# SS2D layer: where the weight and background pools are created relative to the tile pools

## The chip, the core and the metric

The kernel runs on one core of a Trainium2 chip. The metric is the device time of one execution in microseconds (us). The core has five engines that run side by side: PE (matrix multiplies), DVE (VectorE), ACT (ScalarE), POOL (GpSimd) and SP, whose queue issues nearly all transfers here.

## What is computed

Four layers in a row on 8 images of 56 x 56 positions with 128 channels. Layers 0, 2 and 3 are deformable convolutions followed by a small MLP. Layer 1 is the one that the change touches, an SS2D block (a selective scan in four directions). Its core, cut from the reference:

```python
def step(h, t):
    dt_t, u_t, B_t, C_t = t
    h = h * jnp.exp(dt_t[..., None] * A) + (dt_t * u_t)[..., None] * B_t[:, :, None, :]
    y = jnp.einsum('bkdn,bkn->bkd', h, C_t)
    return (h, y)
```

Before the scan stand a layer norm, a projection to 256 channels and a gate, a 3 x 3 depthwise convolution and the projections that give dt, B and C; behind it stand a layer norm, the gate, an output projection and an MLP with 512 hidden channels, each with a residual.

## The kernel before

The layers run one after the other. A layer of deformable convolution (class `Dcn`; layers 2 and 3 share one instance) has two parts per image: a *front*, which loads the image (`xt`, L616), transposes it, makes the projected table (L638, stored by L593), the depthwise convolution (`cv`, L657 and L659), offsets and masks (`om`, L670 to L720) and the list of window addresses (`addr`, L725); and the *sampling*, which builds windows of weights (POOL memset of `win`, L803; ACT hats, L749 and L751; POOL `ay`, L760; DVE `patch`, L809, and `win`, L812) and contracts them on PE. While one image is sampled, the front of the next is interleaved. The first image of an instance has nothing to hide behind but what the layer before leaves.

Layer 1 (class `Vss`) cuts each image into 4 directions x 4 chunks of 784 positions: 128 steps in all, 32 units each. A unit holds 32 channels x 4 states on the 128 partitions and does, in this order: `dA` = exp(dt A) on ACT (L1424), `u` = dt u B on DVE (L1434) or, for every fourth unit, `up` on POOL (L1430), the scan `h` on DVE (L1537), `hc` = h C on POOL (L1542), and PE sums over the states (L1456). The tile `dt` (128 x 2 x 784, three buffers) is fetched by SP (L1364) for every four units. Background generators are advanced by a fixed pace between units: `input_stage` prepares the next image, `output_stage` finishes a chunk of 392 positions (L1235 to L1302: two transfers in, PE steps through a single PSUM buffer `misc`, each emptied by ACT, and one store at L1302). In the last image four output stages are still to be done when the last scan ends.

The weights of the SS2D layer are loaded by ten transfers in `Vss.weights` (L1067) and prepared by small DVE and ACT operations (L1075 to L1114).

The order of work follows from tile pools and a scheduler. A pool takes a contiguous part of each partition's on-chip memory (SBUF), in the order in which pools are created; every tag in it gets its buffers there. Pools of a later layer take the same bytes once the earlier layer has left them, so where a pool lies decides for whose last use its successor waits. In the program as built, the relevant byte ranges per partition are, before the change:

| pool | holds | bytes |
|---|---|---|
| `v_img`, `v_prep` | y, xb, dbl, dd, sp, st, out | 9,408 to 75,520 |
| `v_work` | dt (3 x 6,272), b, c, u, h, hc, up | 75,520 to 163,328 |
| `v_const` | the SS2D weights | 163,328 to 191,008 |
| `v_bg` | the tiles of input_stage and output_stage | 191,008 to 224,096 |

and of the instance for layers 2 and 3, which follows on the same bytes: `c_const` and `c_img` (L501, L502) from 9,408 to 75,040; `c_front` (L503: xt, xT, xp, cv, h and small tiles) from 75,040 to 97,056; `c_block` and `c_tail` (sw, xw, st, X, gelu and others) from 97,056 to 160,928; the unit pools (L775: hat, ay, win, patch) from 160,928 on. PSUM pools are the same before and after.

The functions that the diff touches, and those that call them:

Of the kernel before, what the change touches and what calls it, by code (L numbers as in the profile page):

```python
# [41 lines left out]
F32 = mybir.dt.float32  # L42
# [76 lines left out]
SC, SR = 784, 14  # L119
# [367 lines left out]
class Dcn:  # L487
# [9 lines left out]
    def run(self):  # L497
        tc, nc = self.tc, self.nc
        with ExitStack() as ctx:
            enter = ctx.enter_context  # L500
            self.cp = enter(tc.tile_pool(name="c_const", bufs=1))  # L501
            self.img = enter(tc.tile_pool(name="c_img", bufs=1))  # L502
            self.fp = enter(tc.tile_pool(name="c_front", bufs=1))  # L503
            self.bp = enter(tc.tile_pool(name="c_block", bufs=3))
            self.tp = enter(tc.tile_pool(name="c_tail", bufs=1))
            self.pt = enter(tc.tile_pool(name="c_pt", bufs=3, space=PSUM))
            self.py = enter(tc.tile_pool(name="c_py", bufs=2, space=PSUM))
            self.pm = enter(tc.tile_pool(name="c_pm", bufs=3, space=PSUM))
            self.constants()
            for part in self.parts:  # L510
                part.w = self.net.dcn_weights(part.layer, self.const)
                self.part_constants(part)
                self.split_bias(part)
            self.loop()
            self.check()
        over = nc.values_load(self.net.flag[:1, :1], min_val=0, max_val=1, skip_runtime_bounds_check_because="a comparison's result")
        with tc.If(over > 0):
            for part in self.parts:
                self.net.dcn_slow(part.layer, self.images, part.src, part.dst)
# [513 lines left out]
class Vss:  # L1033
# [8 lines left out]
    def run(self):  # L1042
        tc = self.tc
        with ExitStack() as ctx:
            enter = ctx.enter_context
            self.img = enter(tc.tile_pool(name="v_img", bufs=1))
            self.prep = enter(tc.tile_pool(name="v_prep", bufs=1))
            self.work = enter(tc.tile_pool(name="v_work", bufs=2))
            self.cp = enter(tc.tile_pool(name="v_const", bufs=1))
            self.bg = enter(tc.tile_pool(name="v_bg", bufs=1))  # L1050
            self.dram = enter(tc.tile_pool(name="v_dram", bufs=2, space=DRAM))
            self.pmisc = enter(tc.tile_pool(name="v_misc", bufs=1, space=PSUM))
            self.pdtu = enter(tc.tile_pool(name="v_pdtu", bufs=1, space=PSUM))
            self.pda = enter(tc.tile_pool(name="v_pda", bufs=2, space=PSUM))
            self.pacc = enter(tc.tile_pool(name="v_pacc", bufs=1, space=PSUM))
            self.weights()
            self.scans()
# [300 lines left out]

    def fetch_dt(self, s, cg):

        t = s["dt", cg] = self.work.tile([128, 2, SC], F32, name="dt", tag="dt", bufs=3)
        r = s["dd"]
        src = bass.AP(tensor=r.tensor, offset=r.offset + TC * cg * 2 * SC, ap=[[2 * SC, TC], [0, TS], [1, 2 * SC]])
        self.last_fetch = self.nc.sync.dma_start(out=t.rearrange("p x e -> p (x e)"), in_=src)  # L1364
# [274 lines left out]
```

## Time and profile before

| what | us |
|---|---|
| median of three runs (17844.23 to 17852.9) | 17851.06 |
| the profiled execution's own time | 17839.74 |
| its span, first to last instruction | 17838.2 |
| layer 0, up to the flag check | 0 to 2110 |
| first scan and last scan of layer 1 (L1537) | 2218 and 13404 |
| last store of layer 1 (L1302) | 13583 |
| first window memset of layer 2 (L803) | 13586 |
| end of layers 2 and 3 | 17838 |

Between 3000 and 13000 us, in the middle of layer 1, POOL is busy 9384 of 10000 us, DVE 9104, PE 7951 and ACT 6187. In layers 2 and 3 DVE is the busiest engine and POOL has little to do.

How to read it: the page gives busy times per engine and per group of instructions, with the mean duration of one and the idle time of the engine just before them, and what ended that idle time. A line of a timeline gives start, duration, engine, source line, operation, tiles, and in brackets the idle time before it. SPq lines are issues of transfers on SP's queue.

### The profile page before, as it was taken

What the parts mean: (1) busy time and instruction counts of PE and PEld (TensorE: products, weight loads), DVE (VectorE), ACT (ScalarE), POOL (GpSimd) and SP (SyncE); (2) the same over time, 40 slices, a digit from 0 to 9 for tenths busy, and PEclk for the clock granted to TensorE, in tenths of its full rate; (3) what the DMA queues carried; (4) which work ended last, traced back from release to release, by engine and by line L of the source; (5) the groups of instructions that cost most, each with busy time, mean ns of one, the idle gap of its engine ahead of it and who ended that gap; (6) DMA issues with size and microseconds to landing.
All of it is one profiled execution on the core that took longest, in us unless ns stands there. A gap on an engine that the chain in (4) does not pass through costs nothing. (4 is left out here: it accounts for less than half of the span.)

```text
span 17838.2 us, 255485 instructions
## 1 busy us (share of the span) xinstructions
PE 13881.5 (78%) x90058; PEld 6881.4 (39%) x90058; DVE 15386.3 (86%) x17779; ACT 10928.2 (61%) x19607; POOL 11758.9 (66%) x6462
## 2 busy tenths in 40 slices
PE   5777788788788788788778878878776888777777
PEld 3555522232232233232223223223224666555555
DVE  8888488998998998998898899899996888888886
ACT  4666566566566566566666656656554666666666
POOL 2222189998998998998998999899992111122221
PEclk7788898899899899889888888989887888777778
DMA  7777544444343343343444344344434777777777
GB/s 211 211 204 206 165 153 154 172 169 150 143 159 141 139 163 137 139 165 137 143 162 143 137 158 144 140 155 150 148 134 134 199 198 199 196 210 193 209 196 176
DMA packets 1343087, 2961.69 MB, mean 166 GB/s; under 512 B 90960, under 2 KB 893716, under 8 KB 1327420
## 3 DMA queue, kind: packets, MB, share of 16 engines
q1 hardware_dynamic: 1341788, 2945.17, 52.9%
q8 instruction: 718, 11.76, 0.3%
q14 instruction: 581, 4.76, 0.1%
HBM read 2240.63 MB, written 866.92 MB: 174 GB/s over the span
## 5 line engine op out<-in xcount | busy, mean ns | idle before, releaser
L1542 POOL TENSOR_TENSOR hc<-h,c 128x784 f32<-128x784 f32 x4096 | 7539.5, 1874 | 640.9 <-DVE h L1537 387.9
L1537 DVE TENSOR_TENSOR_SCAN h<-dA,st,u 128x784 f32<-128x784 f32 x3072 | 5579.2, 1840 | 438.9 <-ACT dA L1424 243.2
L1424 ACT ACTIVATE dA<-dt,v_A 128x784 f32<-128x784 f32 x4096 | 3741.9, 915 | 842.2 <-DVE h L1537 827.7
L1456 PE MATMUL acc<-hc,v_sum 128*32 128x392 f32 x16384 | 3148.3, 542 | 103.9 <-POOL hc L1542 103.3
L1434 DVE TENSOR_TENSOR u<-dtu,b 128x784 f32<-128x784 f32 x3072 | 2864.6, 957 | 382.5 <-PE dtu L1418 378.4
L1418 PE MATMUL dtu<-dt,ident 128*128 128x392 f32 x4096 | 2028.2, 626 | 1081.9 <-issue 833.4
L760 POOL TENSOR_TENSOR ay<-hat,om 112x756 f32<-112x756 f32 (+2 forms) x192 | 504.6, 2628 | 2848.6 <-ACT hat L751 2309.7
L1537 DVE TENSOR_TENSOR_SCAN h<-dA,st,up 128x784 f32<-128x784 f32 x1024 | 1876.7, 1833 | 232.0 <-POOL hc L1542 208.6
L1430 POOL TENSOR_TENSOR up<-dt,b 128x784 f32<-128x784 f32 x1024 | 1908.1, 1863 | 79.5 <-DVE h L1537 47.1
L845 ACT COPY st<-pt 128x448 f32<-128x448 f32 (+1 forms) x2240 | 1177.4, 542 | 1201.1 <-PE pt L843 1194.6
L812 DVE TENSOR_TENSOR win<-win,patch 112x252 f32 (+2 forms) x3456 | 1686.4, 501 | 132.2 <-POOL win L803 32.5
L1540 ACT COPY st<-h 128x1 f32<-128x1 f32 x3072 | 582.6, 190 | 1985.3 <-DVE h L1537 1976.8
L843 PE MATMUL pt<-ident,sw 112*128 112x112 f32 (+2 forms) x8960 | 1600.6, 308 | 165.6 <-DMA sw<-skew 165.5
L1456 PEld LDWEIGHTS acc<-hc,v_sum 128*32 128x32 f32 x16384 | 762.0, 116 | 2485.3 <-issue 1656.6
L1418 PEld LDWEIGHTS dtu<-dt,ident 128*128 128x128 f32 x4096 | 860.1, 230 | 2150.6 <-issue 1365.5
L803 POOL MEMSET win<- 128x1820 f32 (+2 forms) x384 | 630.0, 1647 | 1298.4 <-DMA skew<-win 1111.2
L859 PE MATMUL yps<-st,xw 128*32 128x48 f32 (+5 forms) x35840 | 1075.2, 244 | 420.7 <-ACT st L845 414.6
L843 PEld LDWEIGHTS pt<-ident,sw 112*128 112x128 f32 (+2 forms) x8960 | 1113.4, 160 | 441.0 <-issue 156.8
L809 DVE TENSOR_TENSOR patch<-ay,hat 112x756 f32<-112x756 f32 (+2 forms) x1152 | 1225.3, 1070 | 39.5 <-POOL ay L760 36.6
L859 PEld LDWEIGHTS yps<-st,xw 128*32 128x32 f32 (+2 forms) x35840 | 754.1, 125 | 849.5 <-ACT st L845 501.0
L749 ACT ACTIVATE hat<-om,taps 112x252 f32<-112x252 f32 x1280 | 758.6, 730 | 277.2 <-DVE patch L809 261.4
L1448 PE MATMUL acc<-y,ident 128*64 128x392 f32 x1536 | 599.1, 780 | 348.6 <-ACT y L1467 269.5
(193 smaller groups left out, 19827.3 us busy)
## 6 DMA issues: line engine op xcount, KB each, us to landing
dt<-dds SPq DMA_DIRECT2D x1024, 784.0 KB
b<-rows SPq DMA_DIRECT2D x512, 392.0 KB
c<-rows SPq DMA_DIRECT2D x512, 392.0 KB
dds<-dd SPq DMA_DIRECT2D x256, 784.0 KB
sw<-skew SPq DMA_DIRECT2D x224, 812.0 KB
sw<-skew SPq DMA_DIRECT2D x224, 672.0 KB
sw<-skew SPq DMA_DIRECT2D x224, 588.0 KB
skew<-win SPq DMA_DIRECT2D x128, 560.0 KB
```

The source lines that it names most:

```text
L809: nc.vector.tensor_mul(patch[:n], bcast(a, 3, KX), bcast(b, 2, KY))
L812: self.last_add = nc.vector.tensor_add(to, to, patch[:n, NCB * p : NCB * (p + 1)]).ins
L843: last = nc.tensor.transpose(ps[:m, n * g : n * (g + 1)], sw[:n, g, p : p + m], self.net.ident[:n, :n])
L845: nc.scalar.copy(st[:m], ps[:m, : G * n])
L859: self.nc.tensor.matmul(yps[CG * g : CG * (g + 1), t0:t1], lhsT=xw[:m, k + part, CG * g : CG * (g + 1)], rhs=st[:m, at + t0 : at + t1], st ...
L1418: last = nc.tensor.matmul(ps[:, b, :SH], lhsT=self.net.ident, rhs=s["dt", cg][:, 1, SH * b : SH * (b + 1)], start=True, stop=True)
L1424: nc.scalar.activation(da[:, :SC], s["dt", cg][:, 0], AF.Exp, scale=w["A"][:, k, NSG * cg + sg : NSG * cg + sg + 1])
L1430: nc.gpsimd.tensor_mul(u, s["dt", cg][:, 1], s["b", sg])
L1434: nc.vector.tensor_mul(halves[0], s["dtu", cg][:, :, :SH], halves[1])
L1456: nc.tensor.matmul(acc[r : r + TC, :SH], lhsT=w["sum"], rhs=hc[:, SH * b : SH * (b + 1)], start=False, stop=sg == NSG - 1)
L1537: nc.vector.tensor_tensor_scan(hh[:, ::step], dA[:, :SC][:, ::step], u[:, ::step], st[:, t : t + 1], ALU.mult, ALU.add)
L1542: nc.gpsimd.tensor_mul(hc, hh, s["c", sg])
```

## The change

A new pool `v_spread` of three buffers is created where `v_work` was, and holds `dt` alone. `v_const` and `v_bg` follow it, and `v_work`, now without dt, comes after them.

```diff
-            self.work = enter(tc.tile_pool(name="v_work", bufs=2))
+            self.spread = enter(tc.tile_pool(name="v_spread", bufs=3))
             self.cp = enter(tc.tile_pool(name="v_const", bufs=1))
             self.bg = enter(tc.tile_pool(name="v_bg", bufs=1))
+            self.work = enter(tc.tile_pool(name="v_work", bufs=2))
...
-        t = s["dt", cg] = self.work.tile([128, 2, SC], F32, name="dt", tag="dt", bufs=3)
+        t = s["dt", cg] = self.spread.tile([128, 2, SC], F32, name="dt", tag="dt")
```

No operation, tile, size or number of buffers is changed, and dt keeps its bytes (75,520 to 94,336). The new ranges are `v_const` 94,336 to 122,016, `v_bg` 122,016 to 155,104, and `v_work` (b, c, u, h, hc, up) 155,104 to 224,096.

## The prediction

> **What bounds the kernel now.** I read the page first (engines over the span, costliest groups), then the busy times by stage, then the timelines of the two places where layer 1 meets its neighbours.
>
> ```profile
> DVE  8888488998998998998898899899996888888886
> POOL 2222189998998998998998999899992111122221
> ...
> L1542 POOL TENSOR_TENSOR hc<-h,c 128x784 f32<-128x784 f32 x4096 | 7539.5, 1874 | 640.9 <-DVE h L1537 387.9
> L1537 DVE TENSOR_TENSOR_SCAN h<-dA,st,u 128x784 f32<-128x784 f32 x3072 | 5579.2, 1840 | 438.9 <-ACT dA L1424 243.2
> L1430 POOL TENSOR_TENSOR up<-dt,b 128x784 f32<-128x784 f32 x1024 | 1908.1, 1863 | 79.5 <-DVE h L1537 47.1
> ```
>
> Slices 6 to 30 are layer 1. POOL and DVE are both at nine tenths there: each unit costs POOL one hc (1874 ns) and a quarter of an up, and DVE one scan and three quarters of a u. They feed each other through three h buffers, so time saved or lost on POOL passes to the span in large part.
>
> ```profile
> 3000.00:13000.00 10000.00, 7951.28 (x28504) 2821.20 (x28506) 9103.87 (x6877) 6187.12 (x10873) 9383.92 (x5182) 0.89 0.42 150
> 13405.00:13585.00 180.00, 131.46 (x597) 87.20 (x593) 102.50 (x138) 82.83 (x116) 22.91 (x13) 0.85 0.34 99
> ```
>
> The columns are the stretch, its length, busy us (and instructions) of PE, PEld, DVE, ACT and POOL, then clock, DMA share and GB/s. The second row is the gap between the last scan and the first window of layer 2: 180 us in which no engine is full. Two things share it: the four remaining output stages of layer 1, and the front of layer 2's first image.
>
> ```profile
> 13427.09 1.05 SPq L616 DMA_DIRECT2D xt<-x  x2
> ...
> 13455.25 0.71 SPq L1302 DMA_DIRECT2D x<-xt  x1
> ...
> 13499.82 0.33 SPq L1302 DMA_DIRECT2D x<-xt  x1
> ...
> 13541.99 0.35 SPq L1302 DMA_DIRECT2D x<-xt  x1
> ...
> 13582.84 0.35 SPq L1302 DMA_DIRECT2D x<-xt  x1
> ```
>
> ```profile
> 13525.94 0.16 DVE L725 TENSOR_SCALAR addr<-at 1x36 int32<-1x36 f32 x1
> ```
>
> ```profile
> 13585.53 3.88 POOL L803 MEMSET win<- 128x1484 f32 x3 [31.62 <-DMA x<-xt]
> ```
>
> The front starts at 13427 (first L616) and is complete at 13526 (addr), wholly under the output stages. Sampling starts when the last output stage has stored: the memset of win waited for that store, because the unit pools lie on the bytes of v_const and v_bg. So the output stages set the end of this gap, and the front is free.
>
> **The change, part by part.** No operation is added or removed, so everything is order, waits and addresses. In the program as built, the order of every engine and the waits of every unit of layer 1 are the same as before from the second unit to the last scan. Three places differ.
>
> *1. The gap before layer 2.* c_front ends at byte 97,056; the weights now begin at 94,336. They overlap by 2,720 bytes, and the wait is by pool: in the program as built the first load of xt (L616) waits for the last fc2 product of the last output stage (L1297) and the last use of a bias (L1286). It stood before three of the four remaining stores (L1302); now it stands just before the last. Behind it wait its transposes on PE, the copies on ACT, pad on POOL, xp and cv on DVE: the whole front. What becomes earlier is the memset of win (on v_work's bytes now), which gains nothing, since the patches need the front.
>
> New end of the stages: stores are 33.9 us apart when the front barely runs (13421.40, the store before the first of the fence, to 13455.25), 40.9 us in the last stage, where PE has cooled to a granted clock of 0.66. Four stages from 13421.4: 13557 at 33.9, 13585 at 40.9; I take 37 us, as the front no longer takes turns but PE is emptier: 13569. The front took 98.9 us (13427.1 to 13525.9) beside the stages and 101 us in layer 0 (1.5 to 102.9 us) behind cold loads. Its DVE rows in the gap alone (four convolutions of 9.0, xp and om 9, the chain from L675 to L725 about 23, and 11 from load to first cv) make 80; I take 92 alone, ends 80 and 101. From addr to the first patch layer 0 needed 5.3 us (102.7 to 108.0). Sum: 13569 + 92 + 5 = 13666 for the first patch, which was at 13591.3: **+75 us**, ends 13557 + 80 + 5 (+51) and 13585 + 101 + 5 (+100).
>
> *2. What layer 2's second image had ahead.* Under the last stages DVE had also done 22 us of the second image's front (xp, cv from 13526 to 13570). That is now done during sampling. Price between 0 and 22. From the first ay to the second addr took 200 us in layer 0, where nothing was ahead, and 172 here; scaled by the steady spacing of addr (226 in layer 2 against 247 in layer 0) 200 becomes 183, so 11 us: **+11**.
>
> *3. The entry to layer 1.* The weights' bytes were free early (layer 0's windows); now they lie on layer 0's block and tail tiles, so the ten loads move behind the flag check:
>
> ```profile
> 2049.97 0.50 SPq L1067 DMA_DIRECT2D v_tap<-in_v_tap  x1
> ...
> 2055.97 2.56 DVE L1075 TENSOR_TENSOR v_tap<-v_tap,v_in 128x2304 f32<-128x2304 f32 x1 [1.18 <-DMA v_tap<-in_v_tap]
> ...
> 2113.18 23.02 SPq L1193 DMA_DIRECT2D xt<-x  x5
> ...
> 2116.32 0.49 DVE L1128 BATCH_NORM_STATS2 bn_st<-xt 112x6 f32<-112x128 f32 x2 [1.72 <-DMA xt<-x]
> ```
>
> On SP the ten issues take 4.2 us and stand before the first xt load of layer 1. v_tap alone (1.18 MB) needed 6.0 us from issue to use; all ten are 2.4 MB, twice that, and the statistics (L1128) stand behind the weight preparation on DVE and behind the same transfers. The first convolution was at 2131.6, everything in this stretch follows from xt, so the delay is exposed. Ends 4 (issue alone) and 16 (12 for the bytes and 4 for the preparation and one more table load, 1.28); **+10**. What layer 0's tail saves lies in DVE gaps of 14 and 16 us there: 0. The three memsets of xn (1.63 on POOL) are done before xn is written.
>
> *4. Addresses in the middle of layer 1.* b, c, u, h, hc and up move. Matched in order with the program's buffers, the 4096 hc products average 1884.7, 1882.9 and 1879.5 ns in the three lower buffers (bytes 141,376 to 150,784) and 1863.1, 1864.0 and 1867.2 in the upper three; scan and u differ by under 1 ns between their buffers. So the address of POOL's output matters a little. All lower-like: 4096 x 9 ns = +36 us; all upper-like: -36; at the fastest twentieth of the records (1838 for hc, about 1838 for up): 36 x 4096 + 26 x 1024 = -173. Nothing says which: I take **0**.
>
> The Trainium skill, "SBUF — State Buffer", section "Who interferes with whom", names a single cause of contention, the port pair that DVE and GpSimd share, and speaks of no dependence on a tile's offset. By it the fourth term would be exactly 0; the 20 ns between buffers in this trace speak against it, and by those rows the term is -36 to +36.
>
> **Sum** against the profiled execution (17839.7): 75 + 11 + 10 + 0 = +96, 17936. Its time is 11 us below the median of the runs; on the median 17851 the forecast is **17947** (+0.5%). Its own range: 51 + 0 + 4 - 36 = +19 to 100 + 22 + 16 + 36 = +174, 17870 to 18025. About 0.2% (36 us) is what a measurement of this kernel can tell from no change.
>
> **Rivals.**
> *A, POOL gets quicker.* The new bytes of hc and up lie clear of whatever costs the 20 to 40 ns. For it: the spread of hc between buffers, and POOL's 94% in the middle of layer 1. Against it: no buffer of hc, up, dt or b averages under 1859 ns. At the floor of 1838 and full passage, -173 + 96 = -77: 17774. It shows as faster by 0.2% from -132 us on POOL, a mean of L1542 of about 1842 ns. Chance 0.12.
> *B, the gap closes again.* The front is held as the program says, but the stages run faster alone and layers 2 and 3, where DVE is busy about 85%, catch up: 10 + 20 or so, 17880, within 0.2%. Against it: DVE is the limit there and the first image has no slack. Chance 0.12. That the wait by pool isn't real (the front runs as before) would give +10 to +20 and falls in this case.
> *C, addresses get worse* than the lower buffers, by another 20 ns on each hc: 82 us more, about 18030. Chance 0.08.
> The forecast has 0.68.
>
> The range reaches from B's low end to the forecast's high end, 17840 to 18025; A and half of C are left out. Faster 0.12, same 0.12, slower 0.76.
>
> **What would show it.** Right: in the new timeline the first L616 of layer 2 comes after the last fc2 product (about 13570 to 13600 with the entry's delay), no cv between the last scan and there, first patch about 85 us later than before; the ten L1067 behind the first 2110 us and L1128 at about 2126. Hc's mean within 1865 to 1883. Wrong: xt loaded under the output stages; or a mean of hc, up or the scan moved by over 15 ns, which would make the fourth term, not the gap, decide.

## The result, and the profile after

The changed kernel takes **17933.06 us** (median of 6 runs, 17903.32 to 17959.31) against 17848.71 (6 runs, 17838.29 to 17857.72) for the kernel before: ratio 1.0048, 95% interval 1.0035 to 1.0061. It is slower, by about half of one per cent: 84.4 us on the medians. Its profiled execution took 17931.83 us with a span of 17930.3, 92.1 us more than the profiled execution before. Lines of the code behind the change have one more in their number than before (the scan is now L1538, hc L1543, the store L1303, the weights' loads L1068).

First the page of the changed kernel: POOL's and DVE's slices, and the groups with their busy us, the mean ns of one, the idle us before them and what ended it.

```profile
DVE  8888488998998998998898898899995888888886
...
POOL 2221189998998998998998999999981111222221
...
L1543 POOL TENSOR_TENSOR hc<-h,c 128x784 f32<-128x784 f32 x4096 | 7559.8, 1878 | 624.0 <-DVE h L1538 377.3
L1538 DVE TENSOR_TENSOR_SCAN h<-dA,st,u 128x784 f32<-128x784 f32 x3072 | 5581.9, 1841 | 430.1 <-ACT dA L1425 230.1
```

Layer 1 looks as it did: hc takes 1878 ns where it took 1874. The digits hardly move: where layers 1 and 2 meet (slice 31), DVE's falls from 6 to 5, and a few others differ by one. The busy times of the same two stretches as before (columns as there) say more:

```profile
3000.00:13000.00 10000.00, 7946.38 (x28517) 2820.77 (x28518) 9108.03 (x6880) 6188.22 (x10884) 9406.26 (x5184) 0.89 0.42 149
13405.00:13585.00 180.00, 125.56 (x427) 65.71 (x425) 29.03 (x49) 63.93 (x95) 26.58 (x16) 0.80 0.15 41
```

The middle of layer 1 is unchanged within 0.3% on every engine. In the gap, DVE's 102.5 us became 29.0: the front's convolutions are no longer there. The timeline of SP's queue shows why, and then those of DVE and POOL:

```profile
13432.32 0.35 SPq L1303 DMA_DIRECT2D x<-xt  x1
...
13470.00 0.37 SPq L1303 DMA_DIRECT2D x<-xt  x1
...
13507.48 0.33 SPq L1303 DMA_DIRECT2D x<-xt  x1
...
13544.99 0.33 SPq L1303 DMA_DIRECT2D x<-xt  x1
13581.97 0.34 SPq L616 DMA_DIRECT2D xt<-x  x1
13582.52 0.33 SPq L1303 DMA_DIRECT2D x<-xt  x1
```

```profile
13663.44 0.17 DVE L725 TENSOR_SCALAR addr<-at 1x36 int32<-1x36 f32 x1
...
13667.86 1.32 DVE L809 TENSOR_TENSOR patch<-ay,hat 112x525 f32<-112x525 f32 x2 [3.71 <-POOL ay L760]
```

```profile
13438.17 3.88 POOL L803 MEMSET win<- 128x1484 f32 x3 [18.14 <-DVE w_ln L238]
```

Stores and loads stand in the forecast order: the first load of xt for layer 2 (L616) was at 13427, ahead of four stores, and now comes at 13582, just before the last one. The front then runs by itself until addr at 13663. The memset of win, which waited for that last store before, has long been done (13438).

The time by landmarks of the two profiled executions:

| stretch | before | after | difference |
|---|---|---|---|
| start to the flag check (L1030) | 2102.7 | 2106.0 | +3.3 |
| check to first scan | 115.5 | 126.4 | +10.9 |
| first to last scan | 11185.6 | 11183.8 | -1.8 |
| last scan to first patch of layer 2 | 187.5 | 251.7 | +64.2 |
| first patch to second addr of layer 2 | 170.9 | 175.9 | +5.0 |
| second addr to the last operation (L942) | 4068.9 | 4079.4 | +10.5 |

They add to 92.1 us. The first and the last row are no larger than the scatter. Five kernels (the changed one and the four below that change only the strides of h and hc) have their pools at the same places, and among them the check comes at 2090 to 2106 us and the last row is 4062 to 4079; over all thirteen changed kernels that row differs from before by -13.5 to +13.5 us.

### The profile page after: what moved, and what is told of

Read it like the earlier page. It is cut to its first block, busy times and chain, and to the rows that moved or that the text cites. A ratio compares the mean times of both kernels' runs of the same rounds, so it can differ in the third digit from the quotient of the medians.

```text
span 17930.3 us, 255480 instructions
## 1 busy us (share of the span) xinstructions
PE 13911.1 (78%) x90058; PEld 6898.3 (38%) x90058; DVE 15380.8 (86%) x17779; ACT 10913.4 (61%) x19601; POOL 11787.8 (66%) x6462
## 5 line engine op out<-in xcount | busy, mean ns | idle before, releaser
L1543 POOL TENSOR_TENSOR hc<-h,c 128x784 f32<-128x784 f32 x4096 | 7559.8, 1878 | 624.0 <-DVE h L1538 377.3
L1538 DVE TENSOR_TENSOR_SCAN h<-dA,st,u 128x784 f32<-128x784 f32 x3072 | 5581.9, 1841 | 430.1 <-ACT dA L1425 230.1
L1538 DVE TENSOR_TENSOR_SCAN h<-dA,st,up 128x784 f32<-128x784 f32 x1024 | 1877.4, 1833 | 242.0 <-POOL hc L1543 213.9
L859 PE MATMUL yps<-st,xw 128*32 128x48 f32 (+5 forms) x35840 | 1072.9, 244 | 427.1 <-ACT st L845 419.8
L859 PEld LDWEIGHTS yps<-st,xw 128*32 128x32 f32 (+2 forms) x35840 | 753.1, 125 | 858.1 <-ACT st L845 505.9
```

What stands on the lines that cost most here:

```text
L859: self.nc.tensor.matmul(yps[CG * g : CG * (g + 1), t0:t1], lhsT=xw[:m, k + part, CG * g : CG * (g + 1)], rhs=st[:m, at + t0 : at + t1], st ...
L1538: nc.vector.tensor_tensor_scan(hh[:, ::step], dA[:, :SC][:, ::step], u[:, ::step], st[:, t : t + 1], ALU.mult, ALU.add)
L1543: nc.gpsimd.tensor_mul(hc, hh, s["c", sg])
```

## Experiments

The theory is that of the prediction: the front of layer 2 is held because v_const reaches 2,720 bytes into c_front's range, the entry is late because the weights' loads moved behind the flag check, and the addresses in the middle of layer 1 decide little. Each kernel below is the changed one with the edit shown, unless another is named, and none leaves out computation. All ratios are to the kernel before, run beside it.

### The gap: is it the overlap?

**gap_free** pads dt's buffers, so that v_const begins at 97,120, behind c_front's last byte. The order of the pools stays.

```diff
-        t = s["dt", cg] = self.spread.tile([128, 2, SC], F32, name="dt", tag="dt")
+        flat = self.spread.tile([128, 2 * SC], F32, name="dt", tag="dt", padded_shape=[128, 1800])
+        t = s["dt", cg] = flat.rearrange("p (x e) -> p x e", x=2)
```

> The changed kernel, with each dt buffer padded from 6,272 to 7,200 bytes, so that the weights begin at byte 97,120, just past the end of layer 2's front pool (97,056). If the gap is lost because the front's pool overlaps the weights by 2,720 bytes: the front's first load (L616) goes out at about 13440 us again, under the output stages, addr is ready at about 13540, the window memsets (on bytes of the tile pool now) no longer wait for the last store, and the first patch comes at 13545 to 13560 (before 13591, changed kernel 13668). The entry still costs 14 us. Time: 20 to 45 us won in the gap against before, less 14: 0 to 30 us under before, 85 to 115 under the changed kernel. If instead the loss came from addresses in the middle or from the pace of layers 2 and 3: 60 to 90 us over before, as the changed kernel.

Measured: 17833.69 us (11 runs), ratio 0.9988 (0.9979 to 0.9997): 2,784 bytes of padding took the whole loss away and a little more. SP's, POOL's and DVE's timelines of this kernel:

```profile
13436.45 0.35 SPq L1303 DMA_DIRECT2D x<-xt  x1
13442.13 1.05 SPq L616 DMA_DIRECT2D xt<-x  x2
...
13606.48 0.33 SPq L1303 DMA_DIRECT2D x<-xt  x1
```

```profile
13442.30 3.88 POOL L803 MEMSET win<- 128x1484 f32 x3 [18.15 <-DVE w_ln L238]
```

```profile
13540.63 0.17 DVE L725 TENSOR_SCALAR addr<-at 1x36 int32<-1x36 f32 x1
13546.07 1.32 DVE L809 TENSOR_TENSOR patch<-ay,hat 112x525 f32<-112x525 f32 x2 [4.67 <-POOL ay L760]
```

The front runs under the output stages again, as before the change, and the memset of win keeps the early place that the change gave it. So the first patch comes at 13546, 60 us ahead of the last store; before the change it had to wait for that store and stood at 13591. About half of these 45 us last: the first product of sampling (L859) is 24 us early, the second addr 20 us, and the medians differ by 22. (The two profiled executions differ by 6, since the last row of the table is 13.5 us longer here.) The last store slips by 24 us, but 16.5 of these the last scan is late already.

What holds the products back shows on SP's queue. The loads of sw (L826), which bring the windows back for the products, stand behind the last store and wait until it has landed. The second line is from the list of SP's waits between 13565 and 13612 (us in total, times, longest us):

```profile
13608.87 0.88 SPq L826 DMA_DIRECT2D sw<-skew  x1
```

```profile
SPq L826 <- DMA x<-xt: 1.5, 1, 1.5
```

The pool of sw, c_block, begins at byte 97,056, so in this order of pools it lies on the bytes of v_const and v_bg. In all five kernels of this document that have both the front and the windows free, the first product follows the last store by 12 us. No run moves c_block off those bytes, so what that would bring is open.

**weights_alone** and **background_alone** move one pool each: the first leaves v_bg behind v_work, the second leaves v_const there.

```diff
 weights_alone: v_spread, v_const, v_work, v_bg
 background_alone: v_spread, v_bg, v_work, v_const
```

> Pools in the order dt, weights, tiles, background: of the two pools only the weights move ahead of the tiles; the background stays at the end. If the weights are what holds the front and what delays the entry: entry +14 us and gap as in the changed kernel (first L616 of layer 2 just before the last store), the window memsets late again but hidden under the front: +75 to +95 us over before. If the background pool is the cause of either part: the entry or the gap returns to that of before, +14 or +65.

> Pools in the order dt, background, tiles, weights: only the background moves ahead. The weights lie at the end again, on bytes that layer 0 leaves early. If the entry is lost by the ten weight loads: they go out before 2070 us again and the first scan is within 3 us of before (2218). The front's pool now overlaps the background pool, so the wait by pool holds the front until the last output stage has stored: gap +62 to +70, in all +60 to +80 us over before. If only the weights can hold the front, the gap returns and the time is that of before.

Measured: 17945.3 us, ratio 1.0052 (1.0038 to 1.0066), and 17929.34, ratio 1.0045 (1.0031 to 1.0058). Either pool on these bytes holds the front: the first load of xt comes at 13579.1 and 13578.8, the first patch 75.9 and 74.1 us later than before. The entry tells them apart. From check to first scan it is 126.5 us with the weights there and 114.8 with the background there (115.5 before, 126.4 after): the entry's cost belongs to the weights, and v_bg's tiles on layer 0's bytes cost nothing.

### The entry: is it the weights' loads?

Before the change the ten loads were issued at 2040 to 2062 us, under layer 0's last blocks. In the changed kernel they stand between the flag check and the first load of xt:

```profile
2116.95 0.37 SPq L1068 DMA_DIRECT2D v_in<-in_v_in  x1
2117.43 0.36 SPq L1068 DMA_DIRECT2D v_tap<-in_v_tap  x1
...
2124.65 0.33 SPq L1068 DMA_DIRECT2D v_A<-in_v_A  x1
2125.20 0.88 SPq L1194 DMA_DIRECT2D xt<-x  x2
```

**split_weights** is gap_free with two weight pools. What the first units need lies at the top of memory (from byte 208,416); out, fc1, fc2 and small constants lie where v_const was and are loaded after the first fetches. **all_three** is split_weights with h and hc padded (below).

```diff
-            self.cp = enter(tc.tile_pool(name="v_const", bufs=1))
+            self.late = enter(tc.tile_pool(name="v_late", bufs=1))
             self.bg = enter(tc.tile_pool(name="v_bg", bufs=1))
             self.work = enter(tc.tile_pool(name="v_work", bufs=2))
+            self.cp = enter(tc.tile_pool(name="v_const", bufs=1))
...
+        self.late_weights()
```

> The changed kernel with the gap closed, and the weights split: those that the first units of layer 1 need (in, tap, xproj, dt, col, A, dsum, skip, the sum matrix) lie at the top of memory, on bytes that layer 0 doesn't use at its end, and the rest (out, fc1, fc2, the bias and the small constants) is loaded after the first fetches of layer 1. Theory (the 12 to 15 us at the entry are the loads of the weights waiting for layer 0's last tiles): the first scan of layer 1 comes within 4 us of the kernel before, 2214 to 2222 instead of 2232, and the time is 10 to 14 us below the kernel with the gap closed alone, 17820 to 17825. Rival (the entry's time goes to the order of layer 1's first loads and not to the bytes): first scan stays at about 2232, time 17834. Second rival (the late loads stand in the way of the first scans and the start is given back before scan 512): first scan at 2218, scan 512 no earlier than with the gap closed, time 17834.

> The split weights, the closed gap and the padded h and hc together. Theory (the three savings have different places and add): about 17805, 45 to 50 us below the kernel before, ratio 0.9973; first scan at 2214 to 2222, hc at 1854 ns, first patch of layer 2 at about 13520. Rival (the same 14 us are counted twice, since the middle of layer 1 takes up what the entry loses): 17818 to 17824, as the better of the two.

Measured: 17822.07 us, ratio 0.9982 (0.9973 to 0.9991), and 17809.69, ratio 0.9975 (0.9964 to 0.9986). The times came about as expected, but the landmark did not: the first scan stood at 2238.4 and 2231.0, not at 2214 to 2222. Two things were mixed in it. Counted from the check, the statistics of layer 1 (L1128) come 14.4 and 14.3 us later, as before the change (13.7), against 24.9 in the changed kernel; so the eleven microseconds are the loads, as the theory said. But from there to the first scan these kernels need 106.6 and 105.4 us where before it took 101.8, so 4 to 5 us are given back, probably by the late loads; that is not shown, since gap_free, which has none, needs 104.5 us there. And the check itself came late, at 2117.4 and 2111.3. In this layout the early weights' bytes are free from the start, so their loads were issued from 46 us on, among the first transfers of layer 0.

**loads_later** is all_three with those loads queued behind layer 0's last load of X, and with out, its product and the small constants moved to the early pool.

```diff
-                nc.sync.dma_start(out=X[:TB], in_=self.rows_of(...))
+                self.net.last_x = nc.sync.dma_start(out=X[:TB], in_=self.rows_of(...))
...
-            self.weights()
+            with tc.issue_after(self.net.last_x.ins):
+                self.weights()
```

> The kernel with all three cures, with the early weights' loads put on their queue behind the last load of X of layer 0 (about 2028 us) and not at 46 us, and only fc1, fc2 and the bias of fc2 loaded late. In the kernel with all three cures layer 0's first addresses came 4 to 6 us later than in the changed kernel and its check 5 to 11 us later, while the stretch from the check to the first scan was 5 to 7 us shorter. Theory (the early loads stood in the way of layer 0's own first transfers, and the loads behind the check were the entry's cost): first addr back at 102 to 104 us, the check at 2102 to 2107, check to first scan 115 to 118, so the first scan at 2217 to 2225; time 5 to 8 us below all three cures, about 17803, ratio 0.9973. Rival (layer 0's later check was scatter between executions): addr at 107 to 109 or the check at 2110 again, time 17810 or more.

Measured: 17830.28 us, ratio 0.9995 (0.9986 to 1.0004), 11 us below the kernel before that ran beside it, where all_three was 41 us below: a miss. The loads stand where they should (2040 us), the check is at 2103.8 and the first scan at 2223.4, 8 us earlier than in all_three, all of it because the check came earlier. The check to first scan took 119.5 as there (119.7), not 115 to 118, and the first addr of layer 0 was at 105.6. The loss is at the other end: with the larger early pool v_const began at 204,384, and layer 2's unit pools end at 206,228. **loads_free** moves out and its product back to the late pool, so v_const begins at 206,432; nothing else differs from loads_later.

> The kernel with the loads behind layer 0's last X, with out and its product moved back to the late pool, so that the early weights begin at byte 206,432 and not at 204,384; the unit pool of layer 2 ends at 206,228. In the kernel before this one the two overlapped by 1,844 bytes and the first memset of win came at 13586.8 us, behind the last store of the output stages, where it was at 13421 with all three cures. Theory (that overlap of two kilobytes alone took the gain back): first memset of win before 13450, first patch of layer 2 within 10 us behind addr, about 13525 to 13540, first scan of layer 1 at 2218 to 2226, time 17795 to 17812, ratio to the kernel before 0.9970 to 0.9980. Rival (the loads at the end of layer 0, or scatter in the middle of layer 1, took it): first memset early but the time 17820 or more.

Measured: 17804.65 us (8 runs), ratio 0.9973 (0.9962 to 0.9983). The first memset of win in loads_later, and then in loads_free:

```profile
13586.85 5.16 POOL L803 MEMSET win<- 128x1484 f32 x4 [19.34 <-ACT pre L1294]
```

```profile
13436.51 3.88 POOL L803 MEMSET win<- 128x1484 f32 x3 [18.27 <-DVE w_ln L238]
```

An overlap of 1,844 bytes moved that memset by 150 us and the first patch from 13540.1 to 13596.8, and cost some 35 us (11 below the kernel before against 45, each beside its own runs of it; the second addr differs by 34). It is the same mechanism as the change's own, on another pool, and the expectation of loads_later had not seen it. The entry in loads_free: check at 2102.2, first scan at 2222.0. That the loads at 46 us delay layer 0 is likely, not shown: the check came at 2111 and 2117 in the two kernels that have them and at 2090 to 2109 in the twelve that have not, a difference no larger than the scatter among the twelve. The ratio of loads_free can't be told from that of all_three.

### The addresses of h and hc

In the changed kernel v_work lies 60,768 bytes higher and hc's buffers show the same pattern as before: 1894.5, 1895.1 and 1889.7 ns in the three lower ones, 1860.6, 1861.5 and 1863.8 in the upper. What moved with it is only the absolute address; what stayed is the distance from the h that is read to the hc that is written, 9,408 bytes for the lower and 18,816 for the upper three. **phase** gives both tags a stride of 3,200 bytes instead of 3,136.

```diff
-            hh = self.work.tile([128, SC], F32, name="h", tag="h", bufs=3)
+            hh = self.work.tile([128, SC], F32, name="h", tag="h", bufs=3, padded_shape=[128, 800])
...
-            hc = self.work.tile([128, SC], F32, name="hc", tag="hc", bufs=6)
+            hc = self.work.tile([128, SC], F32, name="hc", tag="hc", bufs=6, padded_shape=[128, 800])
```

> The changed kernel with the buffers of h and hc padded from 3,136 to 3,200 bytes (25 x 128). In both kernels hc is slower in its buffers 0 to 2 than in 3 to 5, though their addresses moved by 60,768 bytes; what stayed is the distance from the h that is read to the hc that is written: 9,408 bytes (64 over a multiple of 128) for the first three, 18,816 (a multiple of 128) for the others. If that distance matters: all six average about 1862 ns (changed kernel 1894, 1895, 1890, 1861, 1862, 1864), POOL saves 4096 x 16 ns = 64 us and the time falls by 25 to 64 us against the changed kernel. If it is the turn of the buffer (what PE or DVE does at that time): the pattern of three slow and three quick stays and the time is that of the changed kernel within 15 us.

Measured: all six buffers at 1854 to 1855 ns. The page's group of this kernel:

```profile
L1543 POOL TENSOR_TENSOR hc<-h,c 128x784 f32<-128x784 f32 x4096 | 7486.8, 1855 | 668.3 <-DVE h L1538 395.8
```

Yet the time is 17919.3 us, ratio 1.0039 (1.0026 to 1.0053). That is 14 us below the changed kernel, or 21 when each median is counted from the kernel before that ran beside it, and less than the 25 to 64 expected: hc lost 73 us of busy time, and 44 of these stand in the next column, as idle time of POOL before hc (624.0 became 668.3).

Three kernels then asked which distance it is, with h at 3,136 and only hc's stride changed (3,200; 3,264; 3,168).

> The changed kernel with hc's buffers 3,200 bytes apart and h's still 3,136. The distance from the h that is read to the hc that is written then is, modulo 128 bytes, 64, 0, 64, 64, 0, 64 for the six buffers in turn (in the changed kernel 64, 64, 64, 0, 0, 0; with both padded 0 in all six). Theory (the distance modulo 128 sets the length of the product): hc in order of issue is slow, quick, slow, slow, quick, slow, about 1890 ns and 1857 ns, with a mean of about 1879 ns. Rival (something of the buffer's turn or of its place in the row, such as which buffer is freed when): three slow and then three quick as before, mean 1877 ns. Second rival (only the address of the written buffer counts, or only that of the read one): all six alike, or a pattern of three repeated with another buffer quick. The time is that of the changed kernel within 10 us, 17920 to 17945, whichever holds.

> The changed kernel with hc's buffers 3,264 bytes apart and h's still 3,136. Distances from the h read to the hc written, buffers 0 to 5: 9408, 9536, 9664, 19200, 19328, 19456 bytes. Rule A, read from four kernels (slow where the distance is 192 modulo 256, quick at 0, 64 and 128): buffers 0 and 2 slow (about 1887 ns), the other four quick (about 1856), mean 1866 ns. Rule B (192 modulo 512; the rows so far have no 448): only buffer 0 slow, mean 1861 ns. Rival (no rule of the distance between these two; something else of buffers 0 and 5 in the kernel with hc at 3,200): another set of slow buffers, such as 1 or 4. Time as the changed kernel, 17915 to 17945, whichever holds.

> The changed kernel with hc's buffers 3,168 bytes apart and h's still 3,136, for distances that are no multiple of 64: 9408, 9440, 9472, 18912, 18944, 18976 bytes, modulo 256 these are 192, 224, 0, 224, 0, 32. If only exactly 192 is slow: buffer 0 alone, mean 1861 ns. If the slow distances are a band below a multiple of 256 (the write begins up to 64 bytes before a multiple of 256 from the read): buffers 0, 1 and 3 slow, about 1887 ns each, mean 1872 ns. Rival (the padding to multiples of 64 is what makes a buffer quick): more than three slow. Time as the changed kernel, 17915 to 17945.

The theory that went into hc_padded (distance modulo 128) fell: slow, quick, slow, slow, quick, slow was expected, and two of six were slow. With all rows side by side another rule shows, and the last two kernels were made to test it. Each entry is distance modulo 256: mean ns, buffers 0 to 5 in the order of their addresses:

| kernel | 0 | 1 | 2 | 3 | 4 | 5 |
|---|---|---|---|---|---|---|
| after | 192: 1894.5 | 192: 1895.1 | 192: 1889.7 | 128: 1860.6 | 128: 1861.5 | 128: 1863.8 |
| phase | 128: 1855.2 | 128: 1854.1 | 128: 1855.3 | 0: 1854.2 | 0: 1853.9 | 0: 1854.4 |
| hc_padded | 192: 1887.4 | 0: 1854.1 | 64: 1855.6 | 64: 1856.0 | 128: 1856.5 | 192: 1885.6 |
| hc_3264 | 192: 1879.2 | 64: 1861.0 | 192: 1877.0 | 0: 1858.9 | 128: 1859.8 | 0: 1861.4 |
| hc_3168 | 192: 1877.4 | 224: 1857.6 | 0: 1858.5 | 224: 1858.5 | 0: 1859.1 | 32: 1860.3 |

Only 192 modulo 256 is slow, by 16 to 35 ns within a kernel, and in hc_3264 the distance 9,664 (448 modulo 512) is as slow as 9,408 (192), so the period is 256. 224 is quick, so it is no band up to 256; 160 was not tried. The place of the other input, c, is no rival: c lies at many distances from every hc buffer, and sorted by both distances modulo 256 each group with 192 from h is slower than every other group of its kernel (in after, 1884 to 1902 against 1860 to 1865). Why this distance, the runs don't say. The times (17914.85, 17915.05 and 17909.06 us, one run each) say no more than that nothing large moved; the first and the last lie 5 and 6 us below what was expected of them.

**gap_free_phase** joins gap_free and phase.

> The changed kernel with both cures: dt's buffers padded so that the weights begin behind the last byte of the front's pool, and h and hc padded to 3,200 bytes. Theory (POOL's time in the middle of layer 1 passes to the span for about a sixth, and the two savings add): 14 us below the kernel with the gap closed alone, 17815 to 17822, ratio to the kernel before about 0.9979; hc at 1854 ns; first patch of layer 2 at about 13530. Rival (POOL's saving passes in full once the gap is closed): 90 us less, about 17745. Second rival (the saving goes into the gap before layer 2, where the stages wait for something else): 17830 to 17836, as the gap closed alone.

Measured: 17814.13 us (11 runs), ratio 0.9977 (0.9968 to 0.9986), hc at 1857 ns. So with the gap closed the padding is worth about 14 us as well. Three pairs now differ in the padding alone, and the differences (each median counted from that of the kernel before that ran beside it) are -21 (phase and the changed kernel), -14 (gap_free_phase and gap_free) and -12 (all_three and split_weights), for 80, 58 and 65 us less busy time of hc and up on the pages. The intervals within a pair overlap, but all three agree: about a fifth to a quarter of POOL's saving reaches the span.

## Why the prediction was right, and where it was not

The sign, the mechanism and the place were right. The sum came within 4 us on the profiled execution (+96 forecast, +92.1 measured), but that closeness is luck: its four terms together measured 78.3 us, and the other 13.8 stand in the first and last rows of the table, which are scatter. On the medians the change cost 84.4 us (17933 against a forecast of 17947). By its steps:

1. *The gap before layer 2, +75.* Measured +64.2 from the last scan to the first patch. The end of the stages came as estimated: stores 37.5 us apart for the assumed 37, and the first load of xt 165.8 us behind the last scan where the sum's 13569 meant 165.2. That was in part luck, since 37 lay between two readings that were not what they were taken for. In the stage of 33.9 us the front does not "barely run": from 13421 to 13455 DVE does about ten of its convolution steps and six xp. The clock of 0.66 is the mean of 13550 to 13600; over the last stage itself (13542 to 13583) it is 0.75. The held stages ran at 0.77 to 0.78. (L616 also stood ahead of four stores before, not three; the sum doesn't use that.) The term that was mis-sized is the front alone: 81.4 us (13582.0 to 13663.4) for the assumed 92. The lower end, 80, worked out from the DVE rows in the gap, was nearly exact. The 92 was a middle towards layer 0's 101, but that row has cold loads in it, and 98.9 was measured beside the stages. Addr to first patch took 4.4 for 5.3. The cause is shown: closing the overlap brings the front back, and either of the two pools on those bytes takes it away.
2. *The second image's head start, +11.* Measured +5.0 to the second addr, inside 0 to 22, and +4.6 to +7.0 in all seven kernels whose front is held. No run isolates this term.
3. *The entry, +10.* Measured +10.9 from the check to the first scan. The +14.2 of the first scan itself contains 3.3 us that layer 0 was late already. Shown by background_alone and by the split kernels.
4. *Addresses in the middle of layer 1, 0.* Measured -1.8. The number was right within the scatter, and two of the reasons beside it were wrong. Which buffers are slow does not follow from the address of POOL's output, but from the distance between its input and its output. And "time saved or lost on POOL passes to the span in large part" failed: 80 us less on POOL gave 14 to 21. The floor of 1838 ns for hc was not reached either; with the slow distance gone all buffers stand at 1854.

Rival A therefore was worth less than it was priced: the 23 ns that phase took from hc (1878 to 1855) were over half of the way to that floor, and 80 us less on POOL brought 14 to 21 us, where the rival counted on full passage. Rival B's catch-up in layers 2 and 3 did not come; from the second addr on the changed kernel lost 10.5 us more, within the scatter named above. (DVE is busy 82% from 13600 us to the end, not 85.) Rival C had its chance: hc's slow buffers did get 10 to 12 ns slower, and hc's busy time rose by 20 us (7539.5 to 7559.8), with nothing of it to be seen between the first and the last scan (-1.8 us).

On the Trainium skill's page "SBUF — State Buffer", section "Who interferes with whom": its single rule is that only the port pair shared by DVE and GpSimd causes contention. By it alone term 4 would be zero, and the span agrees within the scatter. The durations do not: 1854 to 1895 ns for the same instruction beside the same work of the other engines, set by a distance in bytes, of which that section says nothing. Here the measurement decides.

What the prediction did not look for is the gain that lay in the change itself. It said that the earlier memset of win "gains nothing, since the patches need the front". That is true as long as the front is held. With the front free as well, the two together take the start of the sampling from behind the last store, and the order of the change with 2,784 bytes of padding beats the kernel before by a tenth of one per cent (0.9988).

## What to carry to other kernels

Where pools of two stages share bytes, compare the byte ranges before the durations: an overlap of two kilobytes can hold the whole next stage, and padding that makes one pool begin behind the other's last byte can be the cheapest cure. Check every later pool on the same bytes, not just the one that is being cured: here the loads of sw stayed behind the last store. When an engine at nine tenths gets quicker, look whether its idle time in the next column grows before counting the gain.

## What was not expected of the hardware

- POOL's product of two tiles (128 x 784, fp32) takes 1877 to 1895 ns when its output begins 192 bytes modulo 256 behind the input h, and 1854 to 1867 at the other distances tried (0, 32, 64, 128, 224), in the five kernels of the table and the kernel before. In the kernel before, three of six hc buffers had that distance.
